# Three experts' first layers as 15 transposed products, run between full matmuls of the fourth

## The chip, the cores and the metric

The kernel runs on one core of a Trainium2 chip. The metric is device time in microseconds. The kernel before took 3172.05 us (median of three runs, 3170.51 to 3175.56). All data are float32.

## The reference, cut to what matters

The model is four residual layers on an image batch of 8 x 384 x 32 x 32: attention with depthwise projections, a mixture of experts, a 7x7 depthwise convolution, and a three-branch mixer. The change lies in the second one:

```
x = x + moe(gn(x))
def moe(x, gate_w, gate_b, w1, b1, w2, b2):        # 4 experts, 384 hidden
    scores = softmax(x_flat @ gate_w + gate_b);  top_v, top_i = top_k(scores, 2)
    coef = ...     # from which experts are in the top two anywhere, and their weights
    hdn = relu(einsum('bchw,edc->ebdhw', x, w1) + b1)
    y   = einsum('ebdhw,eod->ebohw', hdn, w2) + b2
    return einsum('ebohw,ebhw->bohw', y, coef)
```

When every expert is chosen somewhere in both places of the top two, the two weights of each position add to one for every expert, and the layer is the plain sum of the four experts. The kernel computes this sum, checks the condition on the device, and would compute again by token if it didn't hold. After the layer, `gn` (group norm over 12 channels and the image) feeds the third layer.

## The kernel before, in words

Channels are three tiles of 128 partitions (NC = 3), an image is 1024 columns, and the expert layer (`experts`, from L1091) goes through 8 images by 2 halves of 512 columns (HF), written `b, h` in the loop at L1300. The order of instructions on PE, ACT, DVE and POOL is the order in which the program writes them (`manual_schedule` at L1547 with all four engines); each engine works through its own queue in that order, and a waiting instruction holds all behind it.

For each half:

- **First layers.** For each of the 4 experts `e` and 3 hidden tiles `dc` (list TODO) three matmuls of 128x128 weights by 512 columns accumulate in a PSUM tile `ph` (L1306; pool `eh`, 3 buffers), and ACT adds the bias and rectifies into `hs[:, dc, e]` (L1310). Each float32 matmul appears in the profile as two passes.
- **Second layers.** The 384x384 weight matrix by a half is nine blocks by two column quarters of 256 (QF). In place of 18 block products the kernel forms 15 products of sums of weight blocks (`wsum`, made once on POOL at L1196) with sums of blocks of hidden rows (`hs_sum`, made per half on DVE at L1210 from the list HSUMS). Each of the 15 entries of PRODUCTS gives the weight block, the hidden block (a pair is a plain block, a number is a sum or "node") and where the result is added or subtracted. `products` (L1212) accumulates each over the 4 experts in a PSUM tile `p` (L1217; pool `ep`, 4 buffers), and DVE adds it into the residual tile `r` (L1231, and L1233 for the first one into a block). The first eight HSUMS are formed on DVE during the first layers: three experts at a time (768 columns), then the fourth; the last two (nodes 1 and 5, all experts, 1024 columns) after product 8.
- After product 2, ACT normalises the next half (`normed`, tile `xn`, 4 buffers).

Around it: at h = 0 `next_layer` of the image before runs in steps between the first layers' matmuls (L1311 on): statistics of `r` on DVE, group sums on PE, a power on POOL (L295), then three times a normalisation on ACT, a transpose on DVE (L977), two copies of padded rows on POOL (L978, L979) and a write by SP's queue (L1003). `keep_residual` sends `r` out in eight DMAs on SP. At h = 0 the next image is fetched (`residual`), and at h = 1 `add_x` adds the input on DVE (L1115: two SBUF inputs). At h = 1 gating logits are formed (L1284) and transposed (L1295).

## Time and profile before

| what | time |
|---|---|
| median of three runs | 3172.05 us |
| the profiled execution | 3172.27 us, span 3170.5 us |
| TensorE busy, share of the span | 3023.9 us, 95% |
| DVE, ACT, POOL busy | 1694.7, 1190.1, 253.9 us |
| first-layer matmuls of the experts (L1306) | 504.1 us, 1152 passes |
| second-layer products (L1217) | 435.4 us, 1920 passes |
| expert layer, first to last matmul | 1731.2 to 2667.9 us |

"Busy" is the union of the times at which an engine works. A group of the profile is a line of the program with its operation and shapes; its mean is the duration of one instruction, which can overlap with the next on the same engine, so that the distance from start to start (the pitch) is what a row of them costs. In square brackets stands the idle time before an instruction and what ended it.

### The profile page before, as it was taken

The numbers are of one execution on the slowest core, as the hardware profiler recorded it, in microseconds if no ns is written. First come the engines' busy times: TensorE is split into PE (matmuls) and PEld (weight loads), VectorE is DVE, ScalarE is ACT, GpSimd is POOL, SyncE is SP. The second block draws the span as 40 slices with busy tenths as digits, with TensorE's granted clock in tenths as the row PEclk, the third lists the DMA queues.
The fourth block names the chain that finished last, engine by engine and source line by source line (L and its number), as shares of the span: only waits on it lengthen the run. The fifth ranks groups of instructions, "written<-read, shape, count | busy, mean of one in ns | idle before, by whom it ended". The sixth has DMA issues, their size and how long they took to land.

```text
span 3170.5 us, 42235 instructions
## 1 busy us (share of the span) xinstructions
PE 3023.9 (95%) x17740; PEld 1605.6 (51%) x17740; DVE 1694.7 (53%) x2570; ACT 1190.1 (38%) x1356; POOL 253.9 (8%) x415
## 2 busy tenths in 40 slices
PE   4988999999999999999998999999999999886998
PEld 3775434343433334343433576676665666555543
DVE  6998354445444444445445464564554555447164
ACT  3554453535445353535442221212212112446510
POOL 2432000000000000000001100000000000111400
PEclk9999999999999999999999999999999999998999
DMA  6787011011101111011004021121121113867775
GB/s 222 270 280 288 33 41 65 23 62 43 60 25 60 43 43 62 23 62 43 11 25 163 20 64 40 64 64 40 64 64 49 42 44 129 332 223 241 234 226 185
DMA packets 89089, 322.84 MB, mean 102 GB/s; under 512 B 13608, under 2 KB 16000, under 8 KB 84664
## 3 DMA queue, kind: packets, MB, share of 16 engines
q1 hardware_dynamic: 64936, 251.71, 23.5%
q10 hardware_dynamic: 13776, 35.82, 3.6%
q0 software_dynamic: 10176, 32.51, 3.0%
q8 instruction: 141, 2.31, 0.3%
q14 instruction: 60, 0.49, 0.1%
HBM read 211.66 MB, written 111.68 MB: 102 GB/s over the span
## 4 chain that ended last, share of the span: by engine, by line
PE 82%; DVE 8%; DMA 6%; issue 2%; ACT 1%; POOL 1%; SPq 0%; ACTq 0%; POOLq 0%; DVEq 0%
PE ph L1306 16%; PE sc L734 15%; PE av L753 14%; PE p L1217 13%; PE sc L632 7%; PE sc L687 4%; PE sc L809 4%; DMA w<-in_w 3%; DVE stats L213 2%; DVE y L462 2%; PE ps L1783 2%; PE po L2197 1%; PE po L2200 1%; PE po L2208 1%; DVE xt L429 1%
## 5 line engine op out<-in xcount | busy, mean ns | idle before, releaser
L741 ACT ACTIVATE e<-sc 128x1024 f32<-128x1024 f32 x512 | 483.2, 1031 | 608.2 <-PE sc L734 608.1
L1306 PE MATMUL ph<-xn,w 128*128 128x512 f32 x1152 | 504.1, 596 | 3.0 <-ACT xn L315 3.0
L734 PE MATMUL sc<-qT,kT 64*128 64x512 f32 x2048 | 473.9, 602 | 0.0
L753 PE MATMUL av<-e,vT 128*64 128x512 f32 x2048 | 467.8, 599 | 0.0
L1310 ACT ACTIVATE hs<-ph,b 128x512 f32<-128x512 f32 x192 | 131.8, 686 | 705.7 <-PE ph L1306 705.4
L1306 PEld LDWEIGHTS ph<-xn,w 128*128 128x128 f32 x1152 | 218.2, 191 | 264.6 <-issue 258.6
L734 PEld LDWEIGHTS sc<-qT,kT 64*128 64x128 f32 x2048 | 186.9, 186 | 282.0 <-issue 231.1
L753 PEld LDWEIGHTS av<-e,vT 128*64 128x64 f32 x2048 | 135.6, 137 | 316.4 <-issue 316.4
L632 PE MATMUL sc<-y,pw 128*128 128x512 f32 x576 | 249.3, 594 | 0.0
L491 PE MATMUL ps<-xt,wx 64*64 64x256 f32 x3456 | 200.3, 392 | 35.2 <-DVE xt L429 20.1
L1231 DVE TENSOR_TENSOR r<-r,p 128x256 f32<-128x256 f32 x416 | 157.1, 417 | 138.9 <-PE p L1217 138.9
L769 DVE LOAD_MASK_SELECT sm<-av x64 | 0.9, 14 | 417.0 <-PE av L753 417.0
L771 DVE RECIPROCAL inv<-sm 128x512 f32<-128x512 f32 x64 | 214.6, 3353 | 2.2
L491 PEld LDWEIGHTS ps<-xt,wx 64*64 64x64 f32 x3456 | 158.8, 139 | 75.6 <-issue 38.9
L1065 PE MATMUL ps<-xt,wx 64*64 64x256 f32 (+1 forms) x2912 | 159.1, 377 | 22.6 <-ACT wx L1539 11.8
L632 PEld LDWEIGHTS sc<-y,pw 128*128 128x128 f32 x576 | 109.1, 190 | 139.7 <-issue 138.3
L1217 PE MATMUL p<-hs_sum,wsum 128*128 128x256 f32 x768 | 173.6, 379 | 0.0
L1217 PEld LDWEIGHTS p<-hs_sum,wsum 128*128 128x128 f32 x768 | 146.3, 190 | 19.5
L1210 DVE TENSOR_TENSOR hs_sum<-hs,hs_sum 128x768 f32<-128x768 f32 (+1 forms) x192 | 146.9, 779 | 4.9
L1065 PEld LDWEIGHTS ps<-xt,wx 64*64 64x64 f32 x2912 | 109.1, 138 | 70.8 <-ACT wx L1539 14.1
L687 PE MATMUL sc<-pw_v,y 128*128 128x384 f32 x384 | 128.2, 495 | 10.9 <-ACT y L315 10.9
L366 ACT COPY o<-ps 128x2048 f32<-128x2048 f32 x56 | 103.9, 1856 | 81.6 <-PE ps L491 47.4
(320 smaller groups left out, 3246.8 us busy)
## 6 DMA issues: line engine op xcount, KB each, us to landing
raw<-y SPq DMA_DIRECT2D x72, 512.0 KB
y<-raw SPq DMA_DIRECT2D x24, 1536.0 KB
x<-x SPq DMA_DIRECT2D x23, 608.0 KB
xt<-x SPq DMA_DIRECT2D x23, 608.0 KB
w<-in_w ACTq DMA_DIRECT2D x36, 384.0 KB
xn<-in_x SPq DMA_DIRECT2D x24, 512.0 KB
x<-in_x SPq DMA_DIRECT2D x16, 768.0 KB
z<-z POOLq DMA_DIRECT2D x16, 768.0 KB, 4.3
```

Of the source, the lines that this page charges most:

```text
L491: nc.tensor.matmul(ps[64 * d : 64 * d + 64, 2 * i + e, cc], lhsT=w[r, 12 * cc + 6 * e + 3 * d + k, :], rhs=xt0s[ct][r, 16 * d + 4 * u + 2 ...
L632: nc.tensor.matmul(ps[:, h, :], lhsT=w[:, ct, pair, :], rhs=y[:, ct, h * HF : (h + 1) * HF], start=ct == 0, stop=ct == NC - 1,)
L687: nc.tensor.matmul(ps[:, m, :C], lhsT=y[:, ct, (m0 + m) * P : (m0 + m + 1) * P], rhs=pw_v[:, ct, :], start=ct == 0, stop=ct == NC - 1,)
L734: nc.tensor.matmul(sc[:, s, :], lhsT=kTs[b][r, pair, m * P : (m + 1) * P], rhs=qTs[b][r, pair, h * HF : (h + 1) * HF], start=True, stop=True,)
L741: nc.scalar.activation(e, sc, AF.Exp, scale=1.0 if shifted else HD**-0.5)
L753: nc.tensor.matmul(av[64 * s : 64 * s + 64, :], lhsT=vTs[0][:, m, c0 : c0 + 64], rhs=e[:, s, :], start=m == 0, stop=m == N // P - 1,)
L771: nc.vector.reciprocal(inv, sm)
L1065: nc.tensor.matmul(ps[64 * d : 64 * d + 64, 2 * i + e, c % 2, images], lhsT=w[r, d * K7 + k, :], rhs=by_slot(xts[ct])[r, 16 * d + column(c ...
L1210: nc.vector.tensor_add(rows_of(o, hs, s), rows_of(i, hs, s), rows_of(j, hs, s))
L1217: nc.tensor.matmul(ps[:, :QF], lhsT=block(w)[:, e], rhs=rows_of(x, hs, e), start=e == 0, stop=e == E - 1,)
L1231: nc.vector.tensor_tensor(out=o, in0=o, in1=ps[:, :QF], op=op)
L1306: nc.tensor.matmul(ph, lhsT=w1[:, e, ct, dc * P : (dc + 1) * P], rhs=xns[b, h][:, ct, :], start=ct == 0, stop=ct == NC - 1,)
```

## The change

For all halves but the first, the first layers of experts 0, 1 and 2 are computed like the second layers, with 15 products of 256 columns each in place of 9 matmuls of 512, in the transposed form of the same scheme:

- The sums of `xn` blocks are 12 "forms", made on POOL one half ahead (`make_forms`); the sums of `w1` blocks (three experts, 384 columns each) take 13 additions, made once on POOL (`sum_weights`).
- `dual` runs a product into a PSUM tile of `ep` (now 5 buffers; `eh` gives one up) and then the additions listed in DUAL: the results are gathered in nodes and in `hs` by 19 DVE instructions and 2 ACT copies per expert. The nodes live in the slots of `hs_sum` that belong to the fourth expert. Of the 19, four have both inputs in SBUF (the second entries of products 9, 11, 3 and 7 in DUAL); the others read one operand from PSUM. ACT then rectifies the three tiles in place (`rectify`).
- The fourth expert stays as full matmuls (`classical`), two of which stand after the first two products of each of the three experts, three at the end.
- The first eight HSUMS go to POOL, one expert at a time (32 instructions of 256 columns a half). The last two go to POOL when h = 0 and b > 0, and stay on DVE otherwise.
- `next_layer`'s steps (statistics now one tile at a time), the fetch of the next image, `add_x`, `normed` and the forms are hung as jobs on the products: after their number in `at(i, ...)`. Their transposes, copies and DMAs move with them.
- `xn` has 2 buffers. The first half computes all four experts by full matmuls, the fourth first, and forms all its sums on DVE.

```diff
+R15 = 3
+FORMS = (
+    (4, (1, 1), (0, 1), -1),
+    (14, 4, (2, 1), 1),
+    (13, (2, 0), 14, -1),
+    (1, (0, 0), (1, 0), -1),
+    (0, (0, 0), (2, 0), -1),
+    (11, (0, 1), (2, 0), -1),
+    (3, (2, 1), (0, 1), -1),
+    (10, (1, 0), 14, -1),
+    (8, (0, 1), (1, 0), -1),
+    (2, (0, 0), (0, 1), -1),
+    (6, (2, 1), (2, 0), -1),
+    (5, (1, 1), (1, 0), -1),
+)
+PLAIN = {7: (0, 1), 9: (1, 0), 12: (2, 0)}
+DUAL = (
+    (14, ((14, "p14"),)),
+    (10, ((11, "p10"),)),
+    (4, (((1, 1), "p4", 14, 1),)),
+    (13, ((1, "p13", 14, 1),)),
+    (1, (((1, 0), "p1", 1, 1),)),
+    (12, ((9, "p12", 1, 1),)),
+    (0, (((0, 0), "p0", 9, 1),)),
+    (9, ((8, 11, "p9", -1), ((0, 0), (0, 0), 11, 1))),
+    (11, ((6, "p11", 9, 1), ((1, 0), (1, 0), 8, 1))),
+    (8, ((3, "p8", 8, 1),)),
+    (3, (((0, 1), "p3", 6, 1), ((1, 1), (1, 1), 3, 1))),
+    (7, ((10, 6, "p7", -1), (10, 10, 3, 1))),
+    (2, (((2, 0), "p2", 10, 1),)),
+    (6, (((0, 1), (0, 1), "p6", 1), ((2, 1), "p6", 10, 1))),
+    (5, (((1, 1), (1, 1), "p5", 1), ((2, 1), (2, 1), "p5", 1))),
+)
+NODE_AT = {n: i for i, n in enumerate((1, 9, 6, 10, 14, 11, 8, 3))}
+READY = {6: (0,), 5: (1, 2)}
...
+        def pass_on_steps(r, b, s, t, pool):
+
+            for ct in range(NC + 1):
+                if ct:
+                    x = pool.tile([P, 32 * HP], FP, tag="x2", name="x2", bufs=2)
+                    transpose_in(x.rearrange("p (c h) -> p c h", h=HP), xn2)
+                    nc.sync.dma_start(out=x2mem[b][ct - 1], in_=x)
+                if ct < NC:
+                    xn2 = pool.tile([P, N], FP, tag="xn2", name="xn2", bufs=1)
+                    affine(xn2, r[:, ct, :], s[:, ct : ct + 1], t[:, ct : ct + 1])
+                yield
...
-                tc.tile_pool(name="ep", bufs=4, space=PSUM, side="right", reuse_waits="tile")
+                tc.tile_pool(name="ep", bufs=5, space=PSUM, side="right", reuse_waits="tile")
...
-                yield
+                    yield
...
-                xn = xns[b, h] = wq.tile([P, NC, HF], FP, tag="xn", name="xn", bufs=4)
+                xn = xns[b, h] = wq.tile([P, NC, HF], FP, tag="xn", name="xn", bufs=2)
...
+            forms = wq.tile([P, len(FORMS), QF], FP, name="forms")
+            w1sum = wq.tile([P, len(wslot) - 2, R15, P], FP, name="w1sum")
...
+            def block1(n):
...
+            def sum_weights():
+                for o, i, sign, j in [*WSUMS[3:6], *WSUMS[8:10], *WSUMS[:3], *WSUMS[6:8], *WSUMS[10:]]:
+                    first8 = o == 8 and i != 8
+                    nc.gpsimd.tensor_tensor(
+                        out=block1(5 if first8 else o), in0=block1(5 if i == 8 else i), in1=block1(j),
+                        op=ALU.add if sign > 0 else ALU.subtract,
+                    )
...
+            def make_forms(xn, part=slice(0, len(FORMS))):
+                for o, i, j, sign in FORMS[part]:
+                    i, j = (form_of(v, xn) for v in (i, j))
+                    nc.gpsimd.tensor_tensor(
+                        out=forms[:, fslot[o]], in0=i, in1=j,
+                        op=ALU.add if sign > 0 else ALU.subtract,
+                    )
+
+            def rectify(hs, e, m):
+                affine(hs[:, m, e], hs[:, m, e], 1.0, b1[:, e, m : m + 1], AF.Relu)
+
+            def dual(hs, e, xn, part, got):
+
+                def at(n):
+                    if isinstance(n, str):
+                        return got[n][:, :QF]
+                    if isinstance(n, tuple):
+                        return hs[:, n[0], e, n[1] * QF : (n[1] + 1) * QF]
+                    return hs_sum[:, NODE_AT[n], E - 1]
+
+                for n, ops in DUAL[part]:
+                    ps = got[f"p{n}"] = ep.tile([P, HF], FP, tag="p", name="p")
+                    nc.tensor.matmul(
+                        ps[:, :QF], lhsT=block1(PRODUCTS[n][0])[:, e], rhs=form_of(n, xn),
+                        start=True, stop=True,
+                    )
+                    for o, i, *more in ops:
+                        if not more:
+                            nc.scalar.copy(at(o), at(i))
+                            continue
+                        j, sign = more
+                        nc.vector.tensor_tensor(
+                            out=at(o), in0=at(i), in1=at(j), op=ALU.add if sign > 0 else ALU.subtract
+                        )
+                    for m in READY.get(n, ()):
+                        rectify(hs, e, m)
+
+            def classical(hs, e, dcs, xn):
+                for dc in dcs:
+                    ph = eh.tile([P, HF], FP, tag="h", name="ph", bufs=2)
+                    for ct in range(NC):
+                        nc.tensor.matmul(
+                            ph, lhsT=w1[:, e, ct, dc * P : (dc + 1) * P], rhs=xn[:, ct, :],
+                            start=ct == 0, stop=ct == NC - 1,
+                        )
+                        if ct < NC - 1:
+                            yield
+                    rectified(hs, e, dc, ph)
+                    yield
+
+            def rectified(hs, e, dc, ph):
+                nc.scalar.activation(hs[:, dc, e], ph, AF.Relu, bias=b1[:, e, dc : dc + 1])
...
-            def sums(hs, some, s):
+            def sums(hs, some, s, eng=nc.vector):
                 for o, i, j in some:
-                    nc.vector.tensor_add(rows_of(o, hs, s), rows_of(i, hs, s), rows_of(j, hs, s))
-
-            def products(b, h, hs):
+                    eng.tensor_add(rows_of(o, hs, s), rows_of(i, hs, s), rows_of(j, hs, s))
...
-                    if i == 2:
-                        if h == 0:
-                            normed(b, 1)
-                        elif b + 1 < B:
-                            normed(b + 1, 0)
...
-                        sums(hs, HSUMS[-2:], slice(0, E))
+                        begun_all = b > 0 and h == 0
+                        sums(hs, HSUMS[-2:], slice(0, E), nc.gpsimd if begun_all else nc.vector)
+                    for job in jobs.get(i, ()):
+                        job()
...
+                if b < B - 1:
+                    dq = er.tile([P, NC, 2, 1], FP, tag="dq", name="dq")
+                    st = er.tile([P, NC, 3], FP, tag="st", name="st")
+                    keep_residual(r, b)
+                    for ct in range(NC):
+                        moments2(r, b, (ct,), mv, dq)
+                        yield
+                    ps = eh.tile([P, NC, 2, 1], FP, tag="sm", name="gn_ps")
+                    over_groups(ps, dq, range(NC))
+                    yield
+                    norm2(ps, b, range(NC), st)
+                    yield
+                    steps = pass_on_steps(r, b, st[:, :, 0], st[:, :, 1], er)
+                    for _ in steps:
+                        yield
+                    return
                 dq = er.tile([P, NC, 2, 1], FP, tag="dq", name="dq")
                 st = er.tile([P, NC, 3], FP, tag="st", name="st")
-                parts = (range(NC),) if b < B - 1 else (range(2), range(2, NC))
-                cos = (range(NC),) if b < B - 1 else (range(1), range(1, NC))
+                parts = (range(2), range(2, NC))
+                cos = (range(1), range(1, NC))
...
-            ahead, passing = None, None
+            ahead, passing = {}, None
+
+            def fetch_next(b):
+                ahead[b] = residual(b)
+                next(ahead[b])
+
             for b, h in product(range(B), range(2)):
                 hs = ew.tile([P, NC, E, HF], FP, tag="hs", name="hs")
-                gating = logits(b)
-                for k, (e, dc) in enumerate(TODO):
-                    ph = eh.tile([P, HF], FP, tag="h", name="ph", bufs=3)
-                    for ct in range(NC):
-                        nc.tensor.matmul(
-                            ph, lhsT=w1[:, e, ct, dc * P : (dc + 1) * P], rhs=xns[b, h][:, ct, :],
-                            start=ct == 0, stop=ct == NC - 1,
-                        )
-                    nc.scalar.activation(hs[:, dc, e], ph, AF.Relu, bias=b1[:, e, dc : dc + 1])
-                    if h == 0 and passing and k in (0, 2, 3, 4, 5, 6):
-                        next(passing)
-                    if h == 0 and k == 9 and b + 1 < B:
-                        ahead = residual(b + 1)
-                        next(ahead)
-                    if h == 1 and k in (0, 1, 2, 4):
+                xn = xns[b, h]
+                gating = logits(b) if h else iter(())
+                if (b, h) == (0, 0):
+                    for e in (E - 1, *range(E - 1)):
+                        for _ in classical(hs, e, range(NC), xn):
+                            pass
+                        if e == E - 3:
+                            for s in (slice(E - 1, E), slice(0, E - 2)):
+                                sums(hs, HSUMS[:-2], s)
+                    sums(hs, HSUMS[:-2], slice(E - 2, E - 1))
+                    sum_weights()
+                else:
+                    full = classical(hs, E - 1, range(NC), xn)
+                    for e in range(R15):
+                        got = {}
+                        dual(hs, e, xn, slice(0, 2), got)
                         next(gating, None)
-                    if h == 1 and k == 3 and b + 1 < B:
-                        next(ahead)
-                    if k == 9:
-                        sums(hs, HSUMS[:-2], slice(0, E - 1))
-                sums(hs, HSUMS[:-2], slice(E - 1, E))
+                        for _ in range(2):
+                            next(full)
+                        dual(hs, e, xn, slice(2, len(DUAL)), got)
+                        if e:
+                            sums(hs, HSUMS[:-2], slice(e - 1, e), nc.gpsimd)
+                    next(gating, None)
+                    for _ in full:
+                        pass
+                    for e in range(R15 - 1, E):
+                        sums(hs, HSUMS[:-2], slice(e, e + 1), nc.gpsimd)
                 if (b, h) == (B - 1, 1):
                     wqpool.close()
                     begin_layer2(B - 1, er)
-                products(b, h, hs)
+                jobs = {}
+
+                def at(i, job, *args):
+                    jobs.setdefault(i, []).append(lambda: job(*args))
+
+                nxt = (b, 1) if h == 0 else (b + 1, 0)
+                if h == 0:
+                    if passing:
+                        for i in (0, 1, 2, 4, 5, 7, 8, 10, 12):
+                            at(i, next, passing)
+                    at(2, normed, b, 1)
+                    half = len(FORMS) // 2
+                    at(3, lambda b=b: make_forms(xns[b, 1], slice(0, half)))
+                    at(6, lambda b=b: make_forms(xns[b, 1], slice(half, len(FORMS))))
+                    if b + 1 < B:
+                        at(13, fetch_next, b + 1)
+                elif b + 1 < B:
+                    for i in (0, 1, 3):
+                        at(i, next, ahead[b + 1])
+                    at(4, normed, b + 1, 0)
+                    at(5, lambda b=b: make_forms(xns[b + 1, 0]))
+                products(b, h, hs, jobs)
                 if h == 1:
                     passing = next_layer(b)
```

More of the change, by code (lines that the diff above doesn't have):

```diff
@@ L1187, in experts @@
             hs_sum = ew.tile([P, len(HSUMS) - 2, E, QF], FP, name="hs_sum")
+            fslot = {n: i for i, (n, *_) in enumerate(FORMS)}
             lg = ew.tile([P, NT, E], FP, name="lg")
@@ L1198, in experts @@
                 )
+            w1slot = {n: i for i, n in enumerate(n for n in wslot if n not in (8, 9))}
+            def block1(n):
+                n = {8: (1, 1), 9: (2, 0)}.get(n, n)
+                if isinstance(n, tuple):
+                    return w1[:, :R15, n[0], n[1] * P : (n[1] + 1) * P]
+                return w1sum[:, w1slot[n]]
+            def sum_weights():
[5 more added lines that the diff above has]
+                    )
@@ new lines, in form_of @@
+            def form_of(n, xn):
+                n = PLAIN.get(n, n) if isinstance(n, int) else n
+                if isinstance(n, tuple):
+                    return xn[:, n[0], n[1] * QF : (n[1] + 1) * QF]
+                return forms[:, fslot[n]]
+            def make_forms(xn, part=slice(0, len(FORMS))):
[5 more added lines that the diff above has]
+                    )
@@ new lines, in rectify @@
+            def rectify(hs, e, m):
[4 more added lines that the diff above has]
+                        return got[n][:, :QF]
+                    if isinstance(n, tuple):
+                        return hs[:, n[0], e, n[1] * QF : (n[1] + 1) * QF]
[16 more added lines that the diff above has]
+                        rectify(hs, e, m)
@@ L1206, in rows_of, with products @@
                 return hs_sum[:, hslot[n], s]
-            def sums(hs, some, s):
+            def sums(hs, some, s, eng=nc.vector):
                 for o, i, j in some:
-                    nc.vector.tensor_add(rows_of(o, hs, s), rows_of(i, hs, s), rows_of(j, hs, s))
-            def products(b, h, hs):
+                    eng.tensor_add(rows_of(o, hs, s), rows_of(i, hs, s), rows_of(j, hs, s))
+            def products(b, h, hs, jobs):
                 r, begun = rs[b], set()
```

## The prediction

> **What bounds the kernel now.** I read the page first, then the chain of waits around one image of the expert layer, then busy times by stretch, then the groups of instructions, then single lines in order of time.
>
> The page and the chain (start, us, engine, what):
>
> ```profile
> PE 3023.9 (95%) x17740; PEld 1605.6 (51%) x17740; DVE 1694.7 (53%) x2570; ACT 1190.1 (38%) x1356; POOL 253.9 (8%) x415
> ...
> 2208.97 23.28 PE ph L1306 x54
> 2232.25 25.90 PE p L1217 x120
> 2258.15 2.57 PE ph L1306 x6
> 2260.73 1.43 PE pl L1284 x24
> 2262.16 5.35 PE ph L1306 x12
> 2267.51 0.22 PE pt L1295 x2
> 2267.72 23.18 PE ph L1306 x54
> 2290.90 25.90 PE p L1217 x120
> 2316.80 7.72 PE ph L1306 x18
> 2324.53 1.46 PE gn_ps L267 x14
> ```
>
> The pieces follow each other without a gap: one image (two halves) takes 117.0 us and TensorE sets all of it. A matmul appears as two passes. 62.1 us for 144 passes is 0.431 us per 512-column pass, so an expert's first layer (9 matmuls, 18 passes) costs 7.76 us; 25.90/120 is 0.216 us per 256-column pass, 0.432 us per product of one expert. DVE is about half busy there, POOL idle (the stretch of this image's first half):
>
> ```profile
> 2208.97:2267.72 58.75, 58.75 (x219) 37.43 (x220) 31.47 (x58) 13.71 (x19) 2.35 (x7) 1.00 0.18 62
> ```
>
> The columns are PE, PEld, DVE, ACT, POOL busy us, then the granted clock 1.00, DMA share and GB/s. So TensorE work removed here is time saved, as long as no other engine becomes late. Prices of the work the change adds:
>
> ```profile
> 2256.46 1.41 DVE L1231 TENSOR_TENSOR r<-r,p 128x256 f32<-128x256 f32 x4 [1.31 <-PE p L1217]
> 2234.14 2.14 DVE L1210 TENSOR_TENSOR hs_sum<-hs,hs_sum 128x256 f32<-128x256 f32 x5
> 2232.88 2.21 ACT L315 ACTIVATE xn<-r,tb,s 128x512 f32<-128x512 f32 x3
> 2265.55 0.47 ACT L315 ACTIVATE lt<-pl,gate_b 128x256 f32<-128x256 f32 x1
> 2656.22 0.75 POOL L1522 TENSOR_TENSOR w<-w 128x84 f32<-128x84 f32 x2 [79.88 <-DMA w<-in_w]
> 1738.32 1.26 POOL L1196 TENSOR_TENSOR wsum<-w 128x512 f32<-128x512 f32 x1 [4.87 <-DMA r<-z]
> 1739.66 2.60 POOL L1196 TENSOR_TENSOR wsum<-wsum,w 128x512 f32<-128x512 f32 x2
> 1738.42 1.18 DVE L1200 TENSOR_TENSOR badd<-badd,zn_t 128x3 f32<-128x3 f32 x1
> 2689.26 0.52 POOL L979 COPY x<-x 128x96 f32<-128x96 f32 x1
> 2657.52 0.75 DVE L1231 TENSOR_TENSOR r<-r,p 128x256 f32<-128x256 f32 x2 [1.30 <-PE p L1217]
> ```
>
> A 256-column DVE add from PSUM follows the one before every 0.34 us (1.41 for four), 0.43 where each needs the last (2.14/5), 0.42 alone. ACT: 512 columns every 0.70 us, 0.80 alone; 256 from PSUM 0.47. POOL: 0.37 us pitch for 84 columns, 1.29 for 512, hence an estimate of 0.74 for 256 and 2.4 for 1024. The last three lines matter most. A DVE add of 3 elements with both inputs in SBUF took 1.18 us (its like take 0.16) and ended when POOL's 512-column add ended; POOL's copy of 0.28 took 0.52 beside a DVE add with two SBUF inputs. But DVE's adds with one input in PSUM ran at 0.75 for two beside POOL adds at 2657.57.
>
> **The change, part by part** (b is the image, h its half; 15 of 16 halves change).
>
> A. TensorE. Three experts need 15 products, 6.48 us in place of 7.76: 1.28 x 45 = **-58 us**. The moved matmuls of statistics and gating cost the same in either place.
>
> B. First layers: a relay between DVE and ACT. An expert now has 19 DVE adds (before: none), 2 ACT copies and 3 rectifying ACT passes. ACT works in the written order, so the next expert's copy of product 14 stands behind this expert's rectifying, which waits for its last DVE adds; the first DVE add of the next expert needs that copy. From the start of a half: first add at 3.2 us (14, 10, two full matmuls, product 4, 0.2 to be seen); 19 adds paced by TensorE end at 10.4; handover by two rectifying passes and a copy 1.65 (it overlaps the last add); the next two experts run 14 x 0.34 + 4 x 0.43 + 0.42 = 6.9 each. POOL now forms the sums of the expert before meanwhile. Four adds per expert have both inputs in SBUF and meet POOL adds; 0.38, 0.38, 0.05, 0.38 us of waiting, 1.2 together. The last result is at 10.4 + 2 x (1.65 + 8.1) = 29.9. TensorE unhindered ends its products at 24.6; five PSUM buffers (ep 4 to 5) let it run ahead, and its last product waits for the add that ends 3.9 before the last result, so ends at 26.45: 1.9 us late. 15 halves: **+28**. Bounds: no meeting 0.1 (+2), every meeting a full POOL add 2.9 (+44); I take 1.9 because the 1.18 us row shows the wait lasting to POOL's end.
>
> C. h = 0, b from 1 (7 halves): POOL's queue. After expert 2 is rectified (29.9 + 1.2 = 31.1; the sums of expert 1 are done by then, at 28.7) POOL has in order: 16 sums of 256 (11.8), 6 forms (4.4), the power of the statistics (0.85, row of L295), 6 forms (4.4), two sums of 1024 (4.8), about 1.2 waiting for DVE: node 5 stands at 58.6. Product 14 (the last) needs it at 29.1 + 14 x 1.727 = 53.3, where 29.1 is 26.5 plus three full matmuls: 5.4 late, **+38**. DVE's wait for the power lies inside this and the five PSUM buffers cover most of it. Bounds: 0.64 us per 256 (half of 1.29) and no waiting, 0.7 (+5); 0.85 us, 11 (+77). Mine lies on the line through both POOL rows.
>
> D. h = 1, b to 6 (7): add_x, now in products 0, 1 and 3, is three DVE instructions of 1.28 us (L1115 at 128x1024) with two SBUF inputs, at the time POOL makes expert 2's sums: 3.84 us put on POOL. Node 4 of expert 3 comes at 41.75, its matmul could start at 39.0: 2.7, **+19** (bounds 0 and 4.5, +31). The next half's forms end at 58, product 10 needs its form at about 59: nothing, but no margin.
>
> E. h = 1 after such an h = 0 (7): the padded-row copies on POOL now come behind C's sums; the write of the first transposed block goes out on SP at 59.3, about 3.5 to land (before, a buffer was reused within 4.0 of its issue), and the third transpose on DVE must wait for that buffer. The next half's adds start 2.2 late, **+15** (0 to +21). keep_residual's eight DMAs and the fetch of the next image also move on SP; the fetch issues a half earlier than its use, 28 us for 2 MB: nothing, and if it came late DVE would stand.
>
> F. First half, once: 13 weight sums on POOL run against 24 DVE sums; **+6** (0 to +10). Statistics by tile add six DVE instructions of 0.16 to 0.2 per image, beside products: nothing.
>
> Sum: -58 + 28 + 38 + 19 + 15 + 6 = **+48**, taken against the profiled execution's 3172.27 (span 3170.5, and the median is 3172.05): 3220 us.
>
> The Trainium skill, "SBUF — State Buffer", "Who interferes with whom", says that a DVE instruction with two SBUF inputs and a GpSimd instruction that reads SBUF exclude each other for whole instructions, one with a single SBUF input does not; "Perfetto Trace Analysis", "Optimizing Scalar/DVE Operations", warns that moving work between the two may therefore not help. The three rows above show the first; by it the sum stands at +48, and without it it would be the faster case below. The warning would have all moved sums come to nothing, which the trace can't show: POOL was idle here.
>
> **Rivals.**
> 1. Faster: DVE and POOL hardly meet. For: only 4 of 19 adds have two SBUF inputs, and a queue's order may drift them apart. Then B is +2; in C POOL starts at 28.7 and is done 26.25 later, at 54.95, for a product due at 51.5: 3.5 x 7 = 25; D 0, E 10, F 0: -58 + 37 = -21, 3151 us; with the cheapest POOL adds C falls to +5 and E to 7: 3128. It decides from the point where under about a quarter of the meetings cost a wait. Against: POOL's sums are queued without gaps over the adds they meet.
> 2. POOL is the bound: adds of 0.85 us or more. B +44, C +77, D +31, E +21, F +10: +125, 3297 us. For: chained sums (10, 3, 8, 11) each wait for the last. Against: the 512-column chain above kept 1.29.
> 3. The gain and waits cancel (within 0.2%, 6 us, about what a measurement can tell from no change).
>
> **How the numbers follow.** The forecast (+8 to +90) 0.52, POOL as bound beyond that 0.17, hardly meeting 0.26, cancelling 0.05. So faster 0.26, same 0.05, slower 0.69. 3128 to 3300 spans from the cheapest rows with no meeting to the dearest; the forecast's own range is 3180 to 3262.
>
> **What would show it.** A: in each changed half 54 passes of 512 columns have given way to 90 of 256, 0.216 apart. B: gaps at duals' products released by DVE, DVE's two-SBUF adds at 0.5 to 1.1 us. C: TensorE waiting for POOL before products 13 and 14 in h = 0, none there in h = 1. D: a wait for POOL at product 5 in h = 1. E: a transpose waiting for a DMA. It would be wrong if the POOL adds last under 0.6 us, if the two-SBUF adds keep 0.42, or if DVE's adds and ACT's handover are shorter than rows of other shapes say.

## The result, and the profile after

The changed kernel takes 3198.63 us (median of four runs, 3196.13 to 3202.52) against 3173.44 us for the kernel before, measured beside it: 1.0081 times as long, 95% interval 1.0064 to 1.0099, some 25 us slower. The forecast was 3220, slower. The side is right, and the sum is 21 us too high; how it came about is another matter, told below.

The page of the changed kernel, engines and instructions:

```profile
PE 3000.7 (94%) x18280; PEld 1710.7 (54%) x18280; DVE 1907.5 (60%) x3221; ACT 1212.6 (38%) x1446; POOL 807.4 (25%) x1102
```

TensorE's busy time fell by 23 us, not by 58, DVE's rose by 213 and POOL's by 554. The chain through one half with h = 0 (start, us, engine, what), where before there was an unbroken row of PE pieces:

```profile
1973.39 0.86 PE p L1295 x4
1974.26 1.72 PE ph L1314 x4
1975.97 6.47 PE p L1295 x30
...
1989.27 1.21 DVE hs L1304 x2
...
2002.04 1.74 PE p L1344 x8
...
2011.87 1.21 DVE gn_bs L250 x2
2013.10 0.22 DVE gn_mv L1371
2013.34 0.17 DVE dq L311
2013.54 0.71 DVE dq L312
2014.27 0.66 DVE dq L313
2014.93 0.04 issue
2014.97 1.44 PE gn_ps L304 x6
2016.41 19.12 PE p L1344 x80
```

TensorE still works where the chain runs through PE, at the prices forecast (30 passes in 6.47, 0.216 each). Where it runs through DVE, TensorE waits: in the first layers for DVE's additions (L1304), and in the products for the **statistics of the group norm** (L250 to L313). The same place in TensorE's own order (the brackets hold the idle time and what ended it):

```profile
2010.51 0.28 PE L304 MATMUL gn_ps<-dq,gmatA 128*128 128x2 f32 x2
2011.20 0.83 PE L304 MATMUL gn_ps<-dq,gmatA 128*128 128x2 f32 x6 [0.41 <-DVE dq L313]
2014.97 1.44 PE L304 MATMUL gn_ps<-dq,gmatA 128*128 128x2 f32 x6 [2.94 <-DVE dq L313]
2016.27 5.44 PE L1344 MATMUL p<-hs_sum,w 128*128 128x256 f32 x16
```

The group sums now come after product 4, and TensorE stands 3.36 us before them. Then sixteen passes take 5.44 us where they took 3.62 elsewhere. Busy times by stretch tell why; the last three columns are the granted clock, the DMA share and GB/s:

```profile
2012.00:2014.00 2.00, 0.03 (x1) 0.00 (x0) 1.90 (x5) 0.00 (x0) 1.84 (x3) 0.75 0.00 0
2014.00:2016.00 2.00, 1.03 (x5) 1.03 (x6) 1.97 (x6) 0.00 (x0) 1.92 (x4) 0.50 0.00 0
2016.00:2018.00 2.00, 2.00 (x6) 1.73 (x7) 0.36 (x1) 0.00 (x0) 1.84 (x4) 0.50 0.00 0
2018.00:2020.00 2.00, 2.00 (x6) 1.55 (x6) 0.00 (x0) 0.00 (x0) 2.00 (x3) 0.55 0.00 0
2020.00:2022.00 2.00, 2.00 (x11) 1.74 (x11) 1.22 (x6) 0.00 (x0) 0.72 (x2) 1.00 0.00 0
```

During the stand (so this text calls a time in which TensorE is idle) the granted clock fell to 0.50 and stayed there for 6.8 us: six passes in 2 us instead of eleven.

Each half from start of first layers to start of the next, in us, from the starts of TensorE's passes (means; before, 32.75 or 32.46 of first layers and 25.9 of products):

| | before | after | of it first layers | of it products |
|---|---|---|---|---|
| first half | 58.7 | 66.0 | 32.8 | 33.2 |
| h = 1, b to 6 | 58.65 | 57.68 | 30.27 | 27.41 |
| h = 1, the last | 58.81 | 56.31 | 30.25 | 26.06 |
| h = 0, b from 1 | 58.36 | 61.95 | 28.66 | 33.3 (32.8 to 33.8) |

So the halves with h = 1 gain 1.0 each and the last of them 2.5, those with h = 0 lose 3.6, and the first loses 7.3: -7 - 2.5 + 25 + 7.3 = +23. From the first to the last matmul of the expert layer the trace has 959.8 us instead of 936.6, +23.1. The rest of the 26.6 us between the two profiled spans lies outside the layer that was changed (2237.4 us instead of 2233.8). In the twelve profiles of this case that part takes 2231.0 to 2238.0 without following the edits, so nothing can be read from the 3.5; for the same reason halves are compared below, rather than totals alone.

### The profile page after: what moved, and what is told of

The parts are those of the page before. It is cut to its first block, busy times and chain, and to the rows that moved or that the text cites. A ratio compares the mean times of both kernels' runs of the same rounds, so it can differ in the third digit from the quotient of the medians.

```text
span 3197.1 us, 45217 instructions
## 1 busy us (share of the span) xinstructions
PE 3000.7 (94%) x18280; PEld 1710.7 (54%) x18280; DVE 1907.5 (60%) x3221; ACT 1212.6 (38%) x1446; POOL 807.4 (25%) x1102
## 4 chain that ended last, share of the span: by engine, by line
PE 73%; DVE 14%; DMA 5%; POOL 3%; issue 3%; ACT 2%; SPq 0%; ACTq 0%; DVEq 0%; POOLq 0%
PE sc L771 15%; PE av L790 14%; PE p L1344 10%; PE p L1295 7%; PE sc L669 7%; PE sc L724 4%; PE ph L1314 4%; PE sc L846 4%; DVE stats L250 2%; DVE y L499 2%; POOL hs_sum L1337 2%; PE ps L1956 2%; DMA w<-in_w 1%; DVE hs L1304 1%; PE po L2370 1%
## 5 line engine op out<-in xcount | busy, mean ns | idle before, releaser
L1337 POOL TENSOR_TENSOR hs_sum<-hs,hs_sum 128x256 f32<-128x256 f32 (+1 forms) x314 | 266.7, 857 | 19.4
L820 POOL DMA_DIRECT2D att<-att x45 | 23.8, 531 | 979.9 <-DVE att L815 979.9
L352 ACT ACTIVATE hs<-hs,b 128x512 f32<-128x512 f32 x135 | 89.1, 715 | 322.8 <-DVE hs L1304 322.8
L1337 POOL TENSOR_TENSOR hs_sum<-hs 128x256 f32<-128x256 f32 x180 | 132.8, 766 | 293.0 <-ACT hs L352 293.0
L528 PEld LDWEIGHTS ps<-xt,wx 64*64 64x64 f32 x3456 | 156.3, 137 | 76.2 <-issue 38.3
L1295 PE MATMUL p<-forms,w 128*128 128x256 f32 x630 | 174.5, 387 | 7.4 <-DVE hs_sum L1304 6.6
L1304 DVE TENSOR_TENSOR hs<-p,hs_sum 128x256 f32<-128x256 f32 x270 | 113.6, 421 | 83.3 <-PE p L1295 35.6
L1314 PE MATMUL ph<-xn,w 128*128 128x512 f32 x342 | 159.5, 601 | 3.0 <-ACT xn L352 3.0
```

The source lines that it names most:

```text
L528: nc.tensor.matmul(ps[64 * d : 64 * d + 64, 2 * i + e, cc], lhsT=w[r, 12 * cc + 6 * e + 3 * d + k, :], rhs=xt0s[ct][r, 16 * d + 4 * u + 2 ...
L1295: nc.tensor.matmul(ps[:, :QF], lhsT=block1(PRODUCTS[n][0])[:, e], rhs=form_of(n, xn), start=True, stop=True,)
L1314: nc.tensor.matmul(ph, lhsT=w1[:, e, ct, dc * P : (dc + 1) * P], rhs=xn[:, ct, :], start=ct == 0, stop=ct == NC - 1,)
L1337: eng.tensor_add(rows_of(o, hs, s), rows_of(i, hs, s), rows_of(j, hs, s))
```

## The experiments

In all ten only the order of the work, the engine that does it or the number of buffers differs from the changed kernel. Where an edit adds or takes away lines, the numbers of later lines shift a little.

### 1. Group sums and what follows them, later

```diff
-                        for i in (0, 1, 2, 4, 5, 7, 8, 10, 12):
+                        for i in (0, 1, 2, 7, 8, 9, 10, 12, 13):
                             at(i, next, passing)
```

> Edit: at h = 0 the group sums on TensorE and the steps behind them move from products 4, 5, 7, 8, 10, 12 to 7, 8, 9, 10, 12, 13. In the changed kernel's trace the half (b = 2, h = 0) takes 62.1 us, and TensorE, in order, stands at the group sums after product 4 for 4.3 us until DVE has the statistics, its granted clock then 0.50 for about 7 us. Theory 1 (that stand is the loss of h = 0, and nothing is behind it): the half falls by 6.1 us to about 56.0, 7 halves, -43 us: 3156, no stretch at clock 0.50. Theory 2 (my term C, POOL's queue, was hidden behind the stand): node 5 is ready 57.7 us after the half's start and product 14 would be due at 54.3, so 3.4 us come back before products 13 and 14: half 59.4, -19 us: 3180. If neither: 3199.

Measured: 3204.33 us, ratio 1.0103 [1.0086, 1.0119], slower than any of the three expectations. The products at h = 0 fell from 33.3 to 30.3: the stand and the half clock are gone. But the first layers after them rose from 30.25 to 33.95, because DVE's last additions and the transposes now fall into them. TensorE at the end of an h = 0 half, then DVE and POOL there:

```profile
2018.32 1.62 PE L304 MATMUL gn_ps<-dq,gmatA 128*128 128x2 f32 x14
...
2029.16 1.99 PE L1344 MATMUL p<-hs_sum,w 128*128 128x256 f32 x8 [0.48 <-POOL hs_sum L1337]
2033.03 1.97 PE L1344 MATMUL p<-hs_sum,wsum 128*128 128x256 f32 x8 [1.87 <-DVE r L1353]
...
2032.39 0.16 DVE L337 SCALAR_TENSOR_TENSOR st<-st 128x3 f32<-128x3 f32 x1 [8.30 <-POOL st L332]
...
2026.76 4.77 POOL L1337 TENSOR_TENSOR hs_sum<-hs,hs_sum 128x1024 f32<-128x1024 f32 x2
2031.49 0.87 POOL L332 TENSOR_TENSOR st<-fm_b,mhalf 128x3 f32<-128x3 f32 x1
```

The fourteen group sums run in one go. What then appears is 2.35 us of new idle time at products 13 and 14. Only about 0.9 of it is the wait of term C, for POOL's two last sums: 0.48 before product 13, and some 0.4 before product 14, as node 5 is done at 2031.53 and TensorE was free at 2031.15. For the remaining 1.5 TensorE waits for a PSUM tile that DVE has not emptied. DVE had stood 8.30 us for the power, and it was this edit that put the power behind the two sums; in the changed kernel it runs among the forms, ahead of them.

### 2. The last two sums on DVE at h = 0 as well

```diff
-                        begun_all = b > 0 and h == 0
+                        begun_all = False
```

> Edit: the last two sums (nodes 1 and 5) on DVE at h = 0 as well, so POOL's queue ends 4.8 us earlier. Prediction's term C as the cause of the slow halves: -38 us, 3161. Stand at the group sums as the cause: node 5 was ready 2.5 us before its product, so nothing is gained; DVE has 2.5 us more per half beside products: 3199, between 3194 and 3204, the h = 0 half stays at 62.

Measured: 3193.47 us, 1.0071 [1.0053, 1.0089], not told apart from the changed kernel; halves of 57.66 and 61.5 to 62.3, the same as there. (The expert layer takes 958.5 us against 959.8; the rest of the difference lies outside it.) POOL's queue before the last products, on which term C rested, does not set the end while the stand is there: TensorE's idle time in these products is the same 3.36, all of it before group sums.

### 3. Both together

> Edit: both of the edits before. If the POOL queue was hidden behind the stand (theory 2), it is out of the way here: half 56 to 57, -36 to -43 us, 3156 to 3163, well under the moved group sums alone (3180). If theory 1 holds the two agree at 3156. If DVE's load of statistics, transposes and the two sums is the bound, the half stays above 59: 3178 or more.

Measured: 3179.30 us, 1.0025 [1.0014, 1.0035]. The products at h = 0 take 27.5, which is 25.9 plus 1.46 of group sums: nothing is left to wait for there. So two limits lay **one behind the other**: the first edit alone gained 3.0 in these products, the second alone nothing, both 5.8. The half itself, 56.2, is what was expected of both; but the next first layers still take 34.0 instead of 30.25. DVE at that place:

```profile
2022.07 0.58 DVE L326 TENSOR_TENSOR st<-fm_a,ref 128x3 f32<-128x3 f32 x1
2025.54 0.16 DVE L337 SCALAR_TENSOR_TENSOR st<-st 128x3 f32<-128x3 f32 x1 [2.89 <-POOL st L332]
...
2033.91 1.97 DVE L1014 STREAM_TRANSPOSE x<-xn 128x1024 f32<-128x1024 f32 x1
...
2036.72 0.41 DVE L1304 TENSOR_TENSOR hs<-p,hs_sum 128x256 f32<-128x256 f32 x1
```

and TensorE, in the first layers that began at 2027.92:

```profile
2029.96 0.67 PE L1295 MATMUL p<-forms,w 128*128 128x256 f32 x2 [1.45 <-DVE r L1353]
...
2036.85 0.70 PE L1295 MATMUL p<-forms,w 128*128 128x256 f32 x2 [1.14 <-DVE r L1353]
```

DVE waits 2.89 us for the power on POOL, which stands behind the forms. So it does its additions of the last products and three transposes of 1.96 to 2.00 late, and TensorE waits for the PSUM tiles that these additions empty. The first addition of the new half comes 8.8 us after its first pass, where the forecast's B counted 3.2.

### 4. Rectifying after the next expert's copies

```diff
-                    for m in READY.get(n, ()):
-                        rectify(hs, e, m)
+                    later += [(e, m) for m in READY.get(n, ())]
...
+                        rectify_later()
```

> Edit: each expert's three rectifying ACT passes are written after the next expert's copies of products 14 and 10, so ACT's queue no longer holds the copy back. Term B as the relay through ACT's queue: DVE's idle 1.3 us before each next expert's first add goes, the first layers' 1.45 us of lateness per half falls to 0.3 or less, and expert 2's sums start about 2 us earlier on POOL, which takes the 1.2 us wait of product 5 at h = 1: -17 to -28 us, 3171 to 3182. Rival: DVE's own adds and the waits for POOL set the pace (7.85 of 8.2 us an expert): then 0 to -5 us, 3194 to 3199.

Measured: 3197.68 us, 1.0082 [1.0062, 1.0101]: no gain. The first layers at h = 0 went from 28.63 to 28.06 or 27.16, at h = 1 they stayed at 30.25. The first addition of an expert no longer waits 1.36 us for ACT, but

```profile
1992.57 0.42 DVE L1304 TENSOR_TENSOR hs<-p,hs_sum 128x256 f32<-128x256 f32 x1 [0.55 <-PE p L1295]
```

for a product that stands behind two full matmuls in TensorE's order; what was gained there went into longer products at h = 0 (34.1 on the mean). The idle time in them stayed at 3.40, but the half clock now lasted 6.83 us in all seven halves. One half of the handover was taken away, and the other half took its place.

### 5. That, and the two full matmuls apart

```diff
-                        for _ in range(2):
-                            next(full)
-                        dual(hs, e, xn, slice(2, len(DUAL)), got)
...
+                        next(full)
+                        dual(hs, e, xn, slice(2, 9), got, later)
+                        next(full)
+                        dual(hs, e, xn, slice(9, len(DUAL)), got, later)
```

> Edit: the rectifying passes after the next expert's copies, as in the run that did this alone and gained 1 us, and also one of the two full matmuls of each expert moved behind its ninth product. That run pointed to two limits one behind the other: with the copies free DVE waited for product 4 (0.7 to 0.9 us idle) and then fell behind 13 products 0.43 apart, as its run of adds takes 7.7 us. If so, the split run lets DVE keep up: first layers 28.6 to 27.3 at h = 0 and 30.25 to 28.9 at h = 1, -20 us less the 1 already had, 3178 to 3182, with the products' parts unchanged (27.4, 33). If DVE's total over the three experts is the limit, no more than 3 us: 3195 or more.

Measured: 3172.77 us, 1.0003 [0.9993, 1.0013], level with the kernel before. First layers 27.15 at h = 0 and 29.0 at h = 1, which is all that the passes need (18 x 0.431 + 90 x 0.216 = 27.2; gating 1.65 more at h = 1). The products at h = 1 fell to 25.90 too: POOL's sums of expert 2 now begin 0.5 us after the start of these products instead of 1.9, and those of the fourth expert 8.3 instead of 10.5, early enough for product 5. Only the products at h = 0 got dearer (34.0), by the half clock behind the stand:

```profile
2007.41 1.44 PE L304 MATMUL gn_ps<-dq,gmatA 128*128 128x2 f32 x6 [2.86 <-DVE dq L313]
2008.71 6.33 PE L1343 MATMUL p<-hs_sum,w 128*128 128x256 f32 x16
```

### 6. The first half's sums of expert 2 on POOL, ahead of the weight sums

```diff
-                    sums(hs, HSUMS[:-2], slice(E - 2, E - 1))
+                    sums(hs, HSUMS[:-2], slice(E - 2, E - 1), nc.gpsimd)
                     sum_weights()
```

> Edit: in the first half expert 2's eight sums are made on POOL, ahead of the 13 sums of weights, instead of on DVE. Term F (DVE's sums with two SBUF inputs and POOL's sums of weights wait for each other, and TensorE waits for a PSUM buffer at product 5, then runs at half clock): the first half falls from 66.0 to between 59 and 60, -6 to -7 us, 3192. If the 33 us of its products have another cause: unchanged, 3199.

Measured: 3193.53 us, 1.0067 [1.0051, 1.0084]. The first half went from 66.0 to 58.4, and 2.0 of it came back in the next, whose forms are now late:

```profile
1788.54 0.70 PE L1295 MATMUL p<-forms,w 128*128 128x256 f32 x2 [1.39 <-POOL forms L1276]
```

### 7. add_x three products later

```diff
-                    for i in (0, 1, 3):
+                    for i in (5, 6, 7):
                         at(i, next, ahead[b + 1])
-                    at(4, normed, b + 1, 0)
-                    at(5, lambda b=b: make_forms(xns[b + 1, 0]))
+                    at(8, normed, b + 1, 0)
+                    at(8, lambda b=b: make_forms(xns[b + 1, 0]))
```

> Edit: at h = 1 add_x moves from products 0, 1, 3 to 5, 6, 7, with the normalisation and the forms after product 8. Term D (add_x holds up POOL's sums of expert 2): the wait for node 4 before the last pass of product 5 goes, products of h = 1 fall from 27.4 to 25.9, 7 halves, -10 us: 3188. Rival (only shifted: the next half's forms become late): the wait moves to the first layers of h = 0, 28.6 grows by 1.5 or more, 3199 or above.

Measured: 3194.13 us, 1.0075 [1.0059, 1.0092]. The products at h = 1 fell from 27.41 to 25.90 in all seven halves: -10.6. But the products at h = 0 rose to 34.2 on the mean (+0.9 each, +6). The stands were the same, 3.36; but six of the seven halves had 6.83 us of half clock, where the changed kernel had that in four and 3.41 in three. Of this time 6.1 us a half lay behind the stand instead of 4.3, and half of the difference is the 0.9. Net -4.5, as measured.

### 8. Four PSUM buffers for products instead of five

```diff
-                tc.tile_pool(name="ep", bufs=5, space=PSUM, side="right", reuse_waits="tile")
+                tc.tile_pool(name="ep", bufs=4, space=PSUM, side="right", reuse_waits="tile")
...
-                    ph = eh.tile([P, HF], FP, tag="h", name="ph", bufs=2)
+                    ph = eh.tile([P, HF], FP, tag="h", name="ph", bufs=3)
```

> The changed kernel with four PSUM buffers for products in place of five, and three for the full matmuls in place of two. Theory of the prediction, that the fifth buffer lets TensorE run ahead of DVE's additions (its last product waited for the add that is one buffer farther back): first layers longer by about one product's pitch, 0.35 to 0.7 us a half, so 28.63 to 29.2 in h = 0 and 30.25 to 30.8 in h = 1, total 3198 + 15 x 0.5 = 3206 (3203 to 3209). Rival, that TensorE's loss in the first layers is set by the relay alone: unchanged halves, 3197 to 3200.

Measured: 3216.28 us, 1.0146 [1.0125, 1.0167]. The first layers grew by 1.48 in every changed half (30.11 and 31.74), twice to four times what was expected; the products at h = 1 shrank by 1.0, those at h = 0 grew by 0.6, and the first half grew by 1.9. The fifth buffer does cover part of the relay, as the forecast had it, and is worth more than it was thought to be; a third one for the full matmuls does not make up for it.

### 9. All of it

The edits of 5, 6, 7 and 2, and at h = 0 group sums, power and first normalisation after product 7, the three transposes after 9, 11 and 12, the forms after 8 and 10:

```diff
-                        for i in (0, 1, 2, 4, 5, 7, 8, 10, 12):
+                        for i in (0, 1, 2, 7, 7, 7, 9, 11, 12):
...
-                    at(3, lambda b=b: make_forms(xns[b, 1], slice(0, half)))
-                    at(6, lambda b=b: make_forms(xns[b, 1], slice(half, len(FORMS))))
+                    at(8, lambda b=b: make_forms(xns[b, 1], slice(0, half)))
+                    at(10, lambda b=b: make_forms(xns[b, 1], slice(half, len(FORMS))))
```

> Edit: the two edits of the first layers, the first half's, the later add_x, the last two sums on DVE throughout, and at h = 0 group sums, norm and first normalisation together after product 7, the forms after products 8 and 10 (so the power on POOL stands before them), transposes after 9, 11, 12. If the losses found are all: halves near 55.5 (h = 0) and 55.5 (h = 1) against 58.4 and 58.65 before, first half 59: -44 us to the kernel before, about 3128; with one of them left at 2 us per image, 3145. If DVE's sum of work at h = 0 (about 28 us beside 27.4 of TensorE) is the bound, the half after it grows by 3 us: 3150 to 3160.

Measured: 3124.10 us (3121.68 to 3130.58), 0.9857 [0.9841, 0.9874] of the kernel before. **This beats both kernels.** Its halves are 54.61 (h = 0), 55.6 (h = 1; 56.5 for the one after the first half, whose forms are late) and 58.63 (the first). One half with h = 0, products and then the next first layers:

```profile
1994.60 1.89 PE L1343 MATMUL p<-hs_sum,wsum 128*128 128x256 f32 x8
1996.33 1.62 PE L304 MATMUL gn_ps<-dq,gmatA 128*128 128x2 f32 x14
1997.81 3.70 PE L1343 MATMUL p<-hs_sum,wsum 128*128 128x256 f32 x16
...
2015.67 0.70 PE L1295 MATMUL p<-forms,w 128*128 128x256 f32 x2 [0.29 <-DVE r L1352]
```

```profile
1982.50:2010.00 27.50, 27.50 (x136) 24.39 (x135) 24.13 (x52) 5.82 (x8) 22.00 (x30) 1.00 0.06 24
2010.00:2037.10 27.10, 26.81 (x129) 19.96 (x128) 24.39 (x63) 8.57 (x16) 12.79 (x21) 1.00 0.29 105
```

TensorE is busy for all 27.50 us of the products, at clock 1.00. Of 27.10 in the first layers 0.29 is left, and there it waits for DVE, now busy for 24 of 27 us.

### 10. The same with the old relay

The best kernel without the edit of experiment 5.

> The quick version of before (x10) with its relay as in the changed kernel: rectifying right after each product that completes a tile, and both full matmuls after the second product. Everything else as in x10: group sums, norm steps and forms after product 7 and later in h = 0, last two sums on DVE, add_x after products 5 to 7, first half's sums of the third expert on POOL. Theory that a relay costs 1.45 us per half whatever stands behind it (28.63 against 27.19 in h = 0; 30.25 against 28.84 in h = 1, from the changed kernel): first layers 28.6 and 30.3 to 31.0, total 3124 + 14 x 1.2 = 3141 (3136 to 3147). Rival, that a late relay also makes DVE late for what follows it (the additions of the products, the norm steps, the transposes of the next first layers, as in the run with groups later and sums on DVE, where h = 1 took 34.0 in its first layers): total 3165 to 3180, with h = 1's first layers at 33 to 34.

Measured: 3145.38 us (3142.95 to 3148.01), 0.9918 [0.9900, 0.9936]. First layers of 28.64 and 31.12, against 27.15 and 29.71 in the best: 1.4 to 1.5 in each half, 21.3 us in all. The relay costs the same with the stand and without it; it doesn't make later work late. The products at h = 0 take 27.46 in both, so the relay had no part in the stand.

## Why the prediction was right or wrong

Its terms against what the traces show, in us over the whole kernel:

| term | forecast | measured | how |
|---|---|---|---|
| A, fewer passes | -58 | -58 | 15 x 3 x 1.28; the best kernel's h = 0 halves are 54.61 instead of 58.36 |
| B, relay | +28 | +22 | 7 x (28.66 - 27.15) + 8 x (30.27 - 28.84); 28.84 is 27.19 of passes and 1.65 of gating |
| C, late at h = 0 | +38 | +41 | 7 x (33.3 - 25.9 - 1.46), but for another reason |
| D, add_x | +19 | +11 | 7 x (27.41 - 25.90) |
| E, late transposes | +15 | 0 | first layers at h = 1 are longer than their passes by the relay alone |
| F, first half | +6 | +7 | 66.0 - 58.7 |
| sum | +48 | +23 | expert layer +23.1 |

**A held** to the pass. **The place of C is the step that failed.** The forecast had node 5 late on POOL before product 14. In the half shown POOL's last sums were done 57.9 us after its start (forecast 58.6), but TensorE came to product 14 only after 60.4, having stood earlier in the half, at the group sums after product 4. The forecast wrote of them that "the moved matmuls of statistics and gating cost the same in either place", and that statistics by tile cost "nothing" beside products. As work they do; but TensorE's queue is in order too, and what stands in it waits for DVE's statistics. The trace of before held the warning: there, the three tiles' statistics ran from 2317.84 to 2322.75, 4.9 us, and eighteen passes of 512 columns (7.7 us) stood between the last product and the group sums:

```profile
2317.84 1.28 DVE L213 BATCH_NORM_STATS2 gn_bs<-r 128x6 f32<-128x512 f32 x2
...
2322.58 0.17 DVE L276 TENSOR_TENSOR dq<-dq,gn_mv 128x3 f32<-128x3 f32 x1
```

After the move the products up to number 4 stand in TensorE's queue in their place, DVE has its additions of products between the tiles, and the small operations run beside POOL's sums:

```profile
2006.15 0.54 DVE L311 TENSOR_TENSOR dq<-gn_mv,ref 128x1 f32<-128x1 f32 x1
2006.72 0.16 DVE L312 TENSOR_TENSOR dq<-dq 128x1 f32<-128x1 f32 x1
2006.91 0.57 DVE L313 TENSOR_TENSOR dq<-dq,gn_mv 128x1 f32<-128x1 f32 x1
```

Six of the nine small operations took 0.54 to 0.70 instead of 0.16, and the third tile was ready at 2014.93 for a queue that was free at 2012.03. The six together took 2.7 us more than at 0.16; without that, by an estimate from these rows, the third tile would have been ready at 2012.2, and little would be left of the stand. No run takes this part alone away. The forecast had put these operations at 0.16 to 0.2, although its own row of a three-element addition that took 1.18 beside POOL showed that small ones are held up too. Experiment 1 shows how little C's own wait is once the stand is gone: about 0.9 us a half, where 5.4 was forecast; what else came up there, the power that came late, was made by that edit. C's sum came out right only because the stand (3.36) and the half clock (about 2.1), neither of them in the forecast, happened to cost as much. That is luck: a fix aimed at C as forecast, experiment 2, left the halves as they were.

**B: right mechanism, smaller.** The handover is in the trace as forecast (first line: DVE waits for ACT's copy behind the rectifying), and additions with two SBUF inputs are the only slow ones:

```profile
1985.09 0.42 DVE L1304 TENSOR_TENSOR hs<-p,hs_sum 128x256 f32<-128x256 f32 x1 [1.36 <-ACT hs_sum L1301]
...
1987.15 0.41 DVE L1304 TENSOR_TENSOR hs_sum<-hs_sum,p 128x256 f32<-128x256 f32 x1
1987.47 0.59 DVE L1304 TENSOR_TENSOR hs<-hs,hs_sum 128x256 f32<-128x256 f32 x1
...
1989.53 0.96 DVE L1304 TENSOR_TENSOR hs<-hs,hs_sum 128x256 f32<-128x256 f32 x1
```

1.41 to 1.48 a half instead of 1.9: the handover left DVE idle for 1.36, not 1.65, and the four meetings cost 0.59, 0.61, 0.96 and 0.50 less 0.42 each, 0.98 together, not 1.2. Experiment 10 prices the whole term at 21.3. No run parts the handover from the meetings.

This is what the Trainium skill, "SBUF — State Buffer", "Who interferes with whom", says of two SBUF inputs beside GpSimd, and the trace agrees in which instructions are hit (0.41 for one PSUM input, 0.50 to 0.96 for two of SBUF). Even 0.96 is less than an addition of 0.42 that first waits for a whole POOL sum of 0.73.

**D: right place, 1.5 instead of 2.7.** add_x took 1.65, 1.83 and 1.60 instead of 1.28, and POOL's sums were held up in turn:

```profile
2067.49 3.08 POOL L1337 TENSOR_TENSOR hs_sum<-hs 128x256 f32<-128x256 f32 x3 [3.24 <-ACT hs L352]
2070.64 5.54 POOL L1337 TENSOR_TENSOR hs_sum<-hs,hs_sum 128x256 f32<-128x256 f32 x5
```

Without meetings these take 2.10 and 3.83, so 2.7 was put on POOL, where the forecast put 3.84 (all of add_x); experiment 7 takes it away whole.

**E: not in the changed kernel.** The third transpose did wait for its buffer, 1.47 us and released by a DMA, as forecast. But the half had become longer by the stand, so the transpose still began within its products, and seven additions later DVE waited for TensorE again, not TensorE for DVE:

```profile
2034.56 1.99 DVE L1014 STREAM_TRANSPOSE x<-xn 128x1024 f32<-128x1024 f32 x1 [1.47 <-DMA x<-x]
2036.39 2.39 DVE L1353 TENSOR_TENSOR r<-r,p 128x256 f32<-128x256 f32 x7
2040.28 0.42 DVE L1304 TENSOR_TENSOR hs<-p,hs_sum 128x256 f32<-128x256 f32 x1 [1.49 <-PE p L1295]
```

In experiments 1 and 3 DVE was late there, by 3.7 in a half (forecast 2.2), but for the power and not for a DMA, and TensorE lost the time through PSUM tiles emptied late, a wait that the forecast didn't have.

**F held**: DVE's eight sums of 256 columns took 8.1 us beside POOL's weight sums and forms, TensorE stood 4.36 in the products behind them, and the clock fell there too; experiment 6 gave back all of the 7.

Of the rivals, "POOL is the bound" fell: its additions took 0.73, against 0.74 forecast, not 0.85. "Hardly meeting" fell for this kernel, as D alone is 11 us of meetings; the best kernel, at 3124, lies below even the cheapest sum of that rival, 3128.

## What to carry to other kernels

When work is moved, write down for each engine's queue, that of the engine with the most work first, when each moved instruction's input is ready and when the queue comes to it; here a few matmuls of two columns, moved, cost more in a half (5.9) than the three experts saved in it (3.84). Waits that lie one behind another hide each other: test a fix together with the fixes behind it, since here the single edits (experiments 1, 2, 4, 6 and 7) brought from 6 us lost to 5 gained, two pairs (3 and 5) 19 and 26, and all of it 74. A scheme that saves TensorE passes pays only once its handovers (copies, sums, buffers) are early enough for TensorE never to wait; here that was a matter of the order of the steps and of which engine makes a few sums.

## What was not expected of the hardware

**In these products the granted clock fell at each stand of 2.86 us or more, for 3.41 or 6.83 us.** Summed over stretches of half a microsecond in each half's products:

| run, products at | idle in them | time at granted clock 0.50 |
|---|---|---|
| changed kernel, h = 0 | 3.36 | 6.83 (four halves), 3.41 (three) |
| experiment 7, h = 0 | 3.36 | 6.83 (six), 3.41 (one) |
| experiment 4, h = 0 | 3.40 | 6.83 (all seven) |
| experiment 5, h = 0 | 2.98 | 6.83 (all seven) |
| experiment 1, h = 0 | 2.35 | 0 |
| changed kernel, h = 1 | 1.25 | 0 |

The longest single stand was 2.94 us in the first two, 2.86 in the next two and 1.87 in experiment 1. Part of the slow time falls into the stand itself: of 6.8 us in the half shown above, 4.8 lie behind it and cost 2.4. The Trainium skill, "TensorE: Matmul & The Clock Gate", "What's actually happening", has half clock after an idle window of about 3.4 us, the windows running freely. The lengths 3.41 and 6.83, and the same stand giving now one and now two of them, agree with this; so does the distance from each fall to the next in the changed kernel's trace, which is a whole multiple of 3.413 us every time. But here 2.86 us of standing was enough, with only matmuls of two columns beside it.

The length of a stand alone does not decide it: later in the changed kernel's trace, outside the expert layer, one of 3.56 us, before the pass at 2745.04, kept clock 1.00. The twelve traces of the expert layer, cut into steps of 3.413 us that begin with the falls, suggest what does: the time in a step that is free of any pass other than the two-column group sums. A step at full clock with at most 2.02 us of it was followed by full clock, and one with 2.18 us or more by half clock (57 times). A step at half clock was followed by full clock with at most 0.48 us of it, and by half clock with 0.79 or more. There is no exception. Idle time alone does not sort them: a step with 1.23 us of it lost the clock (experiment 2), one with 1.86 kept it (experiment 1). These figures are read from runs made for other ends; no run was made to test them.
